# Graph attention and a routed FFN on one core: five conversions and tiny operations of a block's preparation taken off VectorE

## The chip, the cores and the metric

The kernel runs on one core of a Trainium2 chip. The metric is the device time in microseconds of one execution, as a median over runs. PE is TensorE, DVE is VectorE, ACT is ScalarE, POOL is GpSimd, SP is SyncE. A core's engines run their own instruction queues in order and wait for one another by semaphores.

## The reference

Two layers with residuals are computed over 6250 nodes of 256 features and 100000 edges.

```python
x = x + gat(layernorm(x), [src, dst], W_w, W_b, a)       # 2 heads of 128
x = x + ffn(layernorm(x)[None], W1, b1, Wg, bg, Wd, bd)[0]

# gat: Wh = x @ W_w + W_b; s = Wh.a_src, t = Wh.a_dst
#   e = leaky_relu(s[src] + t[dst]); alpha = softmax of e over the edges of one src
#   h'[n] = sum over edges with src == n of alpha * Wh[dst]   (Wh[n] where there is none)
# ffn: H = gelu(x @ W1 + b1); probs = softmax(H @ Wg + bg) over 8 experts
#   out = probs[e] * (H @ Wd[e] + bd[e]) for the expert e of highest probability
```

## The kernel before

**Sorting and projection.** Ahead of the block loop the edges are packed into 31-bit keys (block of 128 sources, destination, source within the block), sorted along each of 128 partitions, and written to memory (`keys`). The nodes are normalised and projected meanwhile and stored in `table`.

**The block loop.** There are 49 blocks of 128 source nodes. For a block, each partition reads a window of its sorted keys (`window`, an indirect DMA on POOL at column `first[:, b]`). `measure` counts on DVE how many keys of the window belong to the block (`c1`), where the next window begins, how many keys are beyond the twelve that a partition handles itself (`over`, in bfloat16), and the destinations of these twelve (`dsti`). `prefix` sums `over` across partitions with three small matmuls on PE, `prefix_out` copies the sums on ACT into `late` and into the last column of `rest`. `split` puts the surplus keys as exact floating-point numbers in the other columns of `rest`, forms the choice matrix `pick`, and the positions `loc` of the twelve. `gather_late` multiplies `pick` with `rest` on PE; `choose` picks out of the product the surplus key of each slot, and adds three more columns to `dsti` and to `loc`. `spread` transposes `loc` on PE, and sends it through memory to be broadcast (`lbc`). `compare` turns `lbc` into one-hot rows, `factors` multiplies them with the source terms on PE and `factor_sums` reduces these.

`fetch` gathers the fifteen rows a partition needs from `table` (15 indirect DMAs of POOL, in three groups of five). For each group `compare_back` forms one-hot columns `hot` on DVE, `weigh` forms the weights on DVE and multiplies them into the rows, with a copy of the weights by ACT at its end (L833), and `add_up` multiplies `hot` with the rows on PE. Edges into the first 256 nodes (the hot ones) are not gathered, but counted (`pick_pairs`, `count_pairs`), weighed (`scale_terms` on ACT, `weigh_pairs` on DVE) and added (`add_pairs` on PE). `finish` divides and adds the residual on DVE.

**The FFN.** Every four finished blocks make a group: `g_norm` on DVE, `g_xn` on ACT, `g_turn` and `g_hidden` on PE with Gelu on ACT, logits, choice of the expert on DVE, and rows sent to their expert's place in memory (`g_rows`, `g_send`). Full tiles of 128 rows of one expert are then loaded (`w_load`), transposed (`w_turn`, with two copies `half` by ACT), multiplied with that expert's weights (`w_expert`: L1150 for the bias and 16 matmuls of L1152 with addresses from registers), and stored.

**The order.** Every step has a slot and a place within it, written by hand, and all instructions are issued in the order of these two numbers. Block b has base `u = 3 * b`; a slot works on several blocks at once.

```python
            at(u - 6, 46, window, b)
            at(u - 4, 24, measure, b)
            at(u - 4, 43, prefix, b)
            at(u - 3, 5, prefix_out, b)
            at(u - 3, 12, split, b)
            at(u - 3, 33.7, gather_late, b)
            at(u - 2, 16, choose, b)
            at(u - 2, 33.5, spread, b)
            at(u, 33, factors, b)
```

`weigh_pairs` of an older block stands at place 13, right behind `split`; `pick_pairs` at 17, right behind `choose`; `w_turn` at 21 and `g_hidden` at 20; `add_up` at 32, before `factors` and `gather_late`; `compare_back` and `weigh` at 48 and 50.

Of the kernel before, what the change touches and what calls it, by code (L numbers as in the profile page):

```python
# [10 lines left out]
F32 = mybir.dt.float32  # L11
BF16 = mybir.dt.bfloat16
I32 = mybir.dt.int32
U16 = mybir.dt.uint16
AF = mybir.ActivationFunctionType
ALU = mybir.AluOpType
# [7 lines left out]
P = 128  # L24


def of_bits(bits):

    return struct.unpack("<f", struct.pack("<I", bits))[0]
# [7 lines left out]
def common_path(  # L37
# [22 lines left out]
    nc = tc.nc  # L60
# [13 lines left out]
    NB = -(-N // P)  # L74
# [5 lines left out]
    HB, HK = 2, 4  # L80
    HOT = HB * P
    ND, NC, WIN = 12, 3, HK + 40
    NR = WIN - HK - ND
    KS = ES + WIN
# [25 lines left out]
    const = ctx.enter_context(tc.tile_pool(name="const", bufs=1))  # L110
# [37 lines left out]
    bd3 = const.tile([3, NX * C], BF16, name="bd3")  # L148


    first_f = const.tile([P, NB + 1], F32, name="first_f")
    nc.gpsimd.iota(first_f[:, 0:1], pattern=[[0, 1]], base=0, channel_multiplier=KS,
                   allow_small_or_imprecise_dtypes=True)
    first = const.tile([P, NB + 1], I32, name="first")
    iota_bf = const.tile([P, HOT], BF16, name="iota_bf")
    nc.vector.tensor_copy(iota_bf, iota_s[:, :HOT])

# [8 lines left out]
    bias = const.tile([P, C], F32, name="bias")  # L166
# [20 lines left out]
    with ExitStack() as edges:  # L187
# [6 lines left out]
        kp = edges.enter_context(tc.tile_pool(name="keyp", bufs=2))  # L194
# [133 lines left out]
        def first_window():  # L328
            few = sp.tile([P, HK], F32, name="few")
            n = sp.tile([P, 1], F32, name="few_n")  # L330
            nc.vector.tensor_scalar(few, bufs[-1][:, :HK], of_bits(0x40000000 + (HOT << 8)), None,
                                    op0=ALU.is_lt, op1=ALU.add, accum_out=n)
            nc.vector.tensor_add(first_f[:, 0:1], first_f[:, 0:1], n)
            nc.vector.tensor_copy(first[:, 0:1], first_f[:, 0:1])

# [176 lines left out]
        for i, (d, flip) in enumerate(steps):  # L514
# [4 lines left out]
            else:  # L519
                early(t, exchange, bufs[i], bufs[i + 1], d, flip)  # L520
        early(t + 1.02, keep_keys)
        early(t + 1.03, first_window)
        for h in range(2):
            early(60 + h, lambda h=h: nc.sync.dma_start(out=empty[:, h * RD // 2:(h + 1) * RD // 2], in_=blank))
# [91 lines left out]
        win, kept, rows, own, sums, res = {}, {}, {}, {}, {}, {}  # L616
# [11 lines left out]
        def measure(b):  # L628


            w = win[b].bitcast(F32)
            mine = kp.tile([P, WIN - HK], F32, name="mine")
            mark = 0x40000000 + ((b + 1) << 21)
            c1 = cnt[:, b:b + 1]
            c2 = kp.tile([P, 1], F32, name="c2")
            nc.vector.tensor_scalar(mine, w[:, HK:], of_bits(mark), None, op0=ALU.is_lt, op1=ALU.add, accum_out=c1)
            nc.vector.tensor_scalar(mine, w[:, HK:], of_bits(mark + (HOT << 8)), None,
                                    op0=ALU.is_lt, op1=ALU.add, accum_out=c2)
            nc.vector.tensor_scalar(c2, c2, c1, float(HK), op0=ALU.subtract, op1=ALU.min)
            nc.vector.scalar_tensor_tensor(first_f[:, b + 1:b + 2], c1, first_f[:, b:b + 1], c2,  # L640
                                           op0=ALU.add, op1=ALU.add)
            nc.vector.tensor_copy(first[:, b + 1:b + 2], first_f[:, b + 1:b + 2])
            over = kp.tile([P, 1], BF16, name="over")
            nc.vector.tensor_scalar(over, c1, float(-ND), 0.0, op0=ALU.add, op1=ALU.max)
            dsti = kp.tile([P, T], I32, name="dsti", bufs=5)
            nc.vector.tensor_scalar(dsti[:, :ND], win[b][:, HK:HK + ND], 8, 0x1FFF,
                                    op0=ALU.logical_shift_right, op1=ALU.bitwise_and)
            kept[b] = {"over": over, "dsti": dsti}
# [11 lines left out]

        def split(b):
            w = win.pop(b)
            rest_i = kp.tile([P, NR], I32, name="rest_i")
            nc.vector.tensor_single_scalar(rest_i, w[:, HK + ND:], 0x1FFFFF, op=ALU.bitwise_and)
            nc.vector.tensor_scalar(kept[b]["rest"][:, :NR], rest_i, float(1 << 21), None, op0=ALU.add)
            pick = kp.tile([P, NS], F32, name="pick", bufs=1)
            nc.vector.tensor_scalar(pick, iota_s, late[:, b, 0:1], None, op0=ALU.is_ge)
            nc.vector.scalar_tensor_tensor(pick, iota_s, late[:, b, 2:3], pick, op0=ALU.is_lt, op1=ALU.mult)

            place_i = kp.tile([P, HK + ND], I32, name="place_i")  # L670
            nc.vector.tensor_single_scalar(place_i, w[:, :HK + ND], 255, op=ALU.bitwise_and)
            loc = kp.tile([P, T], F32, name="loc", bufs=5)
            nc.vector.scalar_tensor_tensor(loc[:, :ND], iota_r[:, :ND], cnt[:, b:b + 1], place_i[:, HK:],
                                           op0=ALU.is_lt, op1=ALU.mult)

            hot_i = kp.tile([P, HK], I32, name="hot_i")
            nc.vector.tensor_single_scalar(hot_i, w[:, :HK], 8, op=ALU.logical_shift_right)
            pair = kp.tile([P, HK], F32, name="pair")
            nc.vector.tensor_scalar(pair, hot_i, float(0x400000 + (b << 13)), None, op0=ALU.subtract)
            kept[b].update(loc=loc, pick=pick, pair=pair, place=place_i)  # L680
# [67 lines left out]
        def choose(b):  # L748
            k = kept[b]
            loc, dsti = k["loc"], k["dsti"]  # L750
            pk = k["pm"][:, :NC * (NR + 1)].rearrange("p (c r) -> p c r", c=NC)
            col = kp.tile([P, NC], F32, name="col")
            nc.vector.tensor_sub(col, slot_of, pk[:, :, NR])
            hit = kp.tile([P, NC, NR], F32, name="hit")
            nc.vector.tensor_tensor(hit, iota_s[:, :NR].unsqueeze(1).to_broadcast([P, NC, NR]),
                                    col.unsqueeze(2).to_broadcast([P, NC, NR]), op=ALU.is_equal)
            nc.vector.tensor_mul(hit, hit, pk[:, :, :NR])
            got = kp.tile([P, NC], F32, name="got")
            nc.vector.tensor_reduce(got, hit, AX.X, ALU.add)
            got_i = kp.tile([P, NC], I32, name="got_i")  # L760
            nc.vector.tensor_copy(got_i, got)
            nc.vector.tensor_scalar(dsti[:, ND:], got_i, 8, 0x1FFF, op0=ALU.logical_shift_right, op1=ALU.bitwise_and)
            nc.vector.tensor_single_scalar(got_i, got_i, 255, op=ALU.bitwise_and)
            nc.vector.tensor_copy(loc[:, ND:], got_i)

        def spread(b):
            k = kept[b]
# [116 lines left out]
        over = fc.tile([1, 1], F32, name="over")  # L884
# [342 lines left out]
        for k in range(NPH):  # L1227
# [26 lines left out]
            n = (TILES if last else max(0, (rows_in - LAG) // P)) - worked  # L1254
# [25 lines left out]
@with_exitstack  # L1280
def gat_then_ffn_kernel(
    ctx: ExitStack,
    tc: tile.TileContext,
    x: bass.AP,
    src: bass.AP,
    dst: bass.AP,
    W: bass.AP,
    Wb: bass.AP,
    a: bass.AP,
    W1: bass.AP,  # L1290
    b1: bass.AP,
    Wg: bass.AP,
    bg: bass.AP,
    Wd: bass.AP,
    bd: bass.AP,
    out: bass.AP,
):
    keep = ctx.enter_context(tc.tile_pool(name="keep", bufs=1))
    odd = keep.tile([1, 1], I32, name="odd")
    common_path(tc, x, src, dst, W, Wb, a, W1, b1, Wg, bg, Wd, bd, out, odd)  # L1300
    flag = tc.nc.values_load(odd[0:1, 0:1], min_val=0, max_val=1,
                             skip_runtime_bounds_check_because="a flag, 0 or 1")
    with tc.If(flag > 0):
        general_path(tc, x, src, dst, W, Wb, a, W1, b1, Wg, bg, Wd, bd, out)
# [506 lines left out]
```

## Time and profile before

| | |
|---|---|
| median of 3 runs | 1692.44 us (1686.08 to 1697.46) |
| the profiled execution | 1684.62 us, of which the span from first to last instruction is 1682.3 us |
| busy | PE 76%, PE's weight load 57%, DVE 65%, ACT 30%, POOL 52% |
| granted TensorE clock, mean | 0.834 |
| DMA | 264.23 MB, mean 157 GB/s |

The busy shares are means over the whole span. In the timeline a line gives start, duration, engine, line and operation; in square brackets stands how long the engine was idle before it, and what ended that. "issue" there is idle time for which the profile shows no wait.

### The profile page before, as it was taken

Reading aid. Unit: us, or ns where it says so; the run is one execution under the profiler, and the core shown is the slowest. Engines: PE = TensorE matmul, PEld = TensorE weight load, DVE = VectorE, ACT = ScalarE, POOL = GpSimd, SP = SyncE. Lnnn points to the kernel's source line nnn. Section 1 sums busy time; section 2 is a strip of 40 time slices with the busy share of each in tenths; the row PEclk is TensorE's granted clock in tenths of the full one; section 3 lists DMA queues with packets and bytes.
Section 4 is the critical chain, followed back from the end, with each engine's and each line's share of the span. In section 5 each row is a group of like instructions: output and inputs, shape, how many; then the busy total and the mean of one; then the engine's idle time right before and its main releaser. Section 6 shows DMA issues by size and latency. Waiting matters only on the chain. (4 is left out here: it accounts for less than half of the span.)

```text
span 1682.3 us, 22169 instructions
## 1 busy us (share of the span) xinstructions
PE 1271.4 (76%) x6405; PEld 958.1 (57%) x6405; DVE 1090.2 (65%) x3765; ACT 511.2 (30%) x1424; POOL 876.6 (52%) x989
## 2 busy tenths in 40 slices
PE   4764765766857878879778778788798787788687
PEld 3543644444545665655656656656556566566576
DVE  7875766476777676776766866766767676654211
ACT  4850211213223223233232232232332332425221
POOL 0026555465656555645656565556466455554343
PEclk9886767877978888979888888789788797889889
DMA  5656545354545455545545554555455444454473
GB/s 167 187 165 168 164 141 161 109 166 139 148 137 160 139 172 158 175 140 159 148 153 163 158 160 134 176 160 166 138 153 168 141 153 140 154 174 159 167 257 105
DMA packets 119213, 264.23 MB, mean 157 GB/s; under 512 B 24988, under 2 KB 65076, under 8 KB 118940
## 3 DMA queue, kind: packets, MB, share of 16 engines
q0 software_dynamic: 47264, 137.46, 27.6%
q1 hardware_dynamic: 64544, 118.23, 21.9%
q10 hardware_dynamic: 7276, 7.03, 1.3%
q8 instruction: 55, 0.90, 0.2%
q14 instruction: 74, 0.61, 0.1%
HBM read 211.45 MB, written 57.90 MB: 160 GB/s over the span
## 5 line engine op out<-in xcount | busy, mean ns | idle before, releaser
L800 POOL DMA_INDIRECT wg<-table,dsti x735 | 715.8, 974 | 416.8 <-issue 266.8
L840 PE MATMUL p_a<-wg,hot 128*128 128x258 f32 x1470 | 391.4, 416 | 76.2 <-ACT wg L833 42.2
L840 PEld LDWEIGHTS p_a<-wg,hot 128*128 128x128 f32 x1470 | 298.7, 209 | 143.4 <-issue 50.0
L923 PE MATMUL pf<-xT,w_sb 128*128 128x512 f32 (+1 forms) x416 | 213.5, 665 | 32.7 <-ACT xT L915 28.9
L832 DVE TENSOR_TENSOR wg<-wg,fix 128x1280 f32<-128x1280 f32 x147 | 218.9, 1489 | 14.0 <-DVE fix L831 8.0
L1152 PE MATMUL pf<-wd_sb,half 128*128 x880 | 221.7, 408 | 0.9 <-issue 0.9
L1152 PEld LDWEIGHTS pf<-wd_sb,half 128*128 128x128 f32 x880 | 174.4, 203 | 43.0 <-issue 13.7
L923 PEld LDWEIGHTS pf<-xT,w_sb 128*128 128x128 f32 x416 | 87.6, 227 | 127.8 <-issue 93.3
L1066 POOL DMA_INDIRECT by_expert<-row,place_i x47 | 46.9, 997 | 186.3 <-ACT row L1060 74.1
L817 DVE TENSOR_TENSOR hot<-fix,loc 128x640 f32<-128x640 f32 x147 | 120.0, 816 | 32.0 <-ACT wg L833 31.7
L1045 ACT COPY row<-pf 128x512 f32<-128x512 f32 x94 | 53.3, 587 | 255.9 <-PE pf L1044 170.3
L746 PE MATMUL pm<-rest,pick 128*128 128x29 f32 x294 | 56.3, 326 | 93.3 <-DVE wt L718 47.2
L710 ACT ACTIVATE wt<-tm,hot_e 128x128 f32<-128x128 f32 x392 | 125.0, 393 | 0.0
L925 ACT ACTIVATE hT<-pf,b_sb 128x512 f32<-128x512 f32 (+1 forms) x104 | 68.1, 662 | 179.0 <-PE pf L923 102.4
L746 PEld LDWEIGHTS pm<-rest,pick 128*128 128x128 f32 x294 | 52.2, 255 | 97.7 <-issue 95.8
L1044 PE MATMUL pf<-ident,hT 128*128 128x128 f32 x392 | 81.8, 355 | 31.9 <-ACT row L1045 19.5
L833 ACT COPY wg<-fix 128x10 f32<-128x10 f32 x147 | 25.2, 172 | 258.1 <-DVE wg L832 138.0
L1045 ACT COPY half<-pf 128x512 f32<-128x512 f32 x110 | 62.3, 585 | 99.8 <-PE pf L1044 48.3
L1044 PEld LDWEIGHTS pf<-ident,hT 128*128 128x128 f32 x392 | 61.3, 185 | 44.2 <-ACT row L1045 25.7
L771 ACT CAST lT<-pm 15x128 bf16<-15x128 f32 x49 | 12.5, 255 | 234.9 <-PE pm L769 174.0
L858 DVE TENSOR_SCALAR den_all<-p_a 128x2 f32<-128x2 f32 (+1 forms) x49 | 7.7, 157 | 114.9 <-PE p_a L840 108.4
L450 PE MATMUL pf<-w_sb,xT 128*128 128x260 f32 x196 | 60.3, 436 | 20.4 <-ACT xT L444 20.3
(274 smaller groups left out, 1875.1 us busy)
## 6 DMA issues: line engine op xcount, KB each, us to landing
row<-by_expert SPq DMA_DIRECT2D x39, 641.0 KB
lbc<-lrow SPq DMA_DIRECT2D x49, 480.0 KB
tm<-terms SPq DMA_DIRECT2D x49, 256.0 KB
wg<-table,dsti POOLq DMA_INDIRECT x735
wg<-by_expert SPq DMA_DIRECT2D x16, 641.0 KB
wd_sb<-in_L_ffn_Wd_dram SPq DMA_DIRECT2D x8, 1024.0 KB
table<-tb ACTq DMA_DIRECT2D x12, 520.0 KB
xs<-in_x_dram SPq DMA_DIRECT2D x12, 512.0 KB
```

The lines of the kernel that those rows point to most:

```text
L450: nc.tensor.matmul(pW[:, :TW], xT[:, k * P:(k + 1) * P], w_sb[:, k, :], start=(k == 0), stop=(k == KC - 1))
L710: nc.scalar.activation(kept[b]["wt"][:, i, g, h, :], tm[:, i, h, :], AF.Identity, scale=hot_e[:, g, i, h:h + 1])
L746: nc.tensor.matmul(pk[:, c, :], k["pick"][:, c * P:(c + 1) * P], k["rest"], start=True, stop=True)
L800: nc.gpsimd.indirect_dma_start(out=wg[:, t - QS[q], :], out_offset=None, in_=table[:, :], in_offset=bass.IndirectOffsetOnAxis(ap=kept[b][" ...
L817: nc.vector.tensor_tensor(hot[:, :n], iota_ps.unsqueeze(1).to_broadcast([P, n, P]), kept[b]["loc"][:, QS[q]:QS[q + 1]].unsqueeze(2).to_bro ...
L832: nc.vector.tensor_mul(wgv[:, :, :, :D], wgv[:, :, :, :D], p_w.unsqueeze(3).to_broadcast([P, n, H, D]))
L840: nc.tensor.matmul(sums[b], hot[:, t - QS[q], :], wg[:, t - QS[q], :SE], start=(t == 0), stop=(t == T - 1))
L923: nc.tensor.matmul(ph[:, :w], wt["w1"][:, k, j * P:(j + 1) * P], xT[:, k, :w], start=(k == 0), stop=(k == KC - 1))
L925: nc.scalar.activation(hT[:, j, :w], ph[:, :w], AF.Gelu, bias=wt["b1"][:, j:j + 1])
L1044: nc.tensor.transpose(pT[:, j * P:(j + 1) * P], rows(4 * h + j), ident)
L1045: nc.scalar.copy(o, pT)
L1152: nc.tensor.matmul(py[:, :C], res[k]["half", i, j // 4][:, j % 4, :], wt["wd"][:, ds(wo[0] + j * C, C)], start=False, stop=(j == KH - 1))
```

## The change

Three functions of a block's preparation change, and the one that finds the first window.

- `first`, the integer column of the next window, is written directly by the operation that computes it. The floating-point copy `first_f` and the conversion after it go, in `measure` and in `first_window`.
- `over` is computed by ACT as Relu(c1 - 12) with a bias tile `minus_nd`, where DVE computed max(c1 - 12, 0).
- In `split` the surplus keys become floating-point numbers by setting the exponent bits (0x4B000000, the value is then 2^23 plus the 21-bit key), in the same operation that masks them, where a second one had added 2^21 and converted.
- In `choose` the bits of the chosen number are used as they are, with no conversion to an integer. The position is masked into a tile of its own, `late_i`, and ACT copies it as a floating-point number into `loc`, where DVE did.

The order of the steps, slots and places stays as it is.

```diff
-    first_f = const.tile([P, NB + 1], F32, name="first_f")
-    nc.gpsimd.iota(first_f[:, 0:1], pattern=[[0, 1]], base=0, channel_multiplier=KS,
+    row_at = const.tile([P, 1], F32, name="row_at")
+    nc.gpsimd.iota(row_at, pattern=[[0, 1]], base=0, channel_multiplier=KS,
                    allow_small_or_imprecise_dtypes=True)
     first = const.tile([P, NB + 1], I32, name="first")
+    minus_nd = const.tile([P, 1], F32, name="minus_nd")
+    nc.gpsimd.memset(minus_nd, float(-ND))
...
-            nc.vector.tensor_add(first_f[:, 0:1], first_f[:, 0:1], n)
-            nc.vector.tensor_copy(first[:, 0:1], first_f[:, 0:1])
+            nc.vector.tensor_add(first[:, 0:1], row_at, n)
...
-            nc.vector.scalar_tensor_tensor(first_f[:, b + 1:b + 2], c1, first_f[:, b:b + 1], c2,
+            nc.vector.scalar_tensor_tensor(first[:, b + 1:b + 2], c1, c2, first[:, b:b + 1],
                                            op0=ALU.add, op1=ALU.add)
-            nc.vector.tensor_copy(first[:, b + 1:b + 2], first_f[:, b + 1:b + 2])
             over = kp.tile([P, 1], BF16, name="over")
-            nc.vector.tensor_scalar(over, c1, float(-ND), 0.0, op0=ALU.add, op1=ALU.max)
+            nc.scalar.activation(over, c1, AF.Relu, bias=minus_nd)
...
-            rest_i = kp.tile([P, NR], I32, name="rest_i")
-            nc.vector.tensor_single_scalar(rest_i, w[:, HK + ND:], 0x1FFFFF, op=ALU.bitwise_and)
-            nc.vector.tensor_scalar(kept[b]["rest"][:, :NR], rest_i, float(1 << 21), None, op0=ALU.add)
+            nc.vector.tensor_scalar(kept[b]["rest"].bitcast(I32)[:, :NR], w[:, HK + ND:], 0x1FFFFF, 0x4B000000,
+                                    op0=ALU.bitwise_and, op1=ALU.bitwise_or)
...
-            got_i = kp.tile([P, NC], I32, name="got_i")
-            nc.vector.tensor_copy(got_i, got)
+            got_i = got.bitcast(I32)
             nc.vector.tensor_scalar(dsti[:, ND:], got_i, 8, 0x1FFF, op0=ALU.logical_shift_right, op1=ALU.bitwise_and)
-            nc.vector.tensor_single_scalar(got_i, got_i, 255, op=ALU.bitwise_and)
-            nc.vector.tensor_copy(loc[:, ND:], got_i)
+            late_i = kp.tile([P, NC], I32, name="late_i")
+            nc.vector.tensor_single_scalar(late_i, got_i, 255, op=ALU.bitwise_and)
+            nc.scalar.copy(loc[:, ND:], late_i)
```

## The prediction

> **What bounds the kernel now.** I read the page's busy shares first, then busy time by stretch, then the groups of the lines that change, then the instructions in order of time over one period of the block loop.
>
> ```profile
> PE 1271.4 (76%) x6405; PEld 958.1 (57%) x6405; DVE 1090.2 (65%) x3765; ACT 511.2 (30%) x1424; POOL 876.6 (52%) x989
> ...
> 900.00:1100.00 200.00, 161.41 (x862) 124.96 (x860) 141.46 (x488) 58.96 (x162) 115.09 (x121) 0.83 0.50 153
> ...
> 926.00:947.00 21.00, 14.76 (x88) 11.95 (x86) 17.87 (x64) 5.65 (x17) 13.44 (x14) 0.97 0.63 197
> 947.00:959.00 12.00, 9.58 (x43) 8.07 (x44) 10.05 (x35) 2.72 (x6) 4.82 (x5) 0.50 0.24 66
> ```
>
> Columns of the stretches: length, then PE, PEld, DVE, ACT, POOL busy with counts, clock, DMA share, GB/s. No engine is full. Over 200 us of the loop PE has 161 and DVE 141, so the bound changes hands along in-order queues. Two stretches of one period show it: from 926 to 947 DVE is busy 17.9 of 21 us and PE only 14.8; right after, PE works at clock 0.50.
>
> The loop repeats every four blocks: `choose` starts its first removed conversion at 811.77 and again at 927.92, 116.15 us later. Between the first `choose` (about 119 us) and the last (1480 us) the pattern settled after about 165 us, so (1480-165)/116.15 = 11.3 periods count.
>
> What the change touches, in the groups by line (name of the operation, then busy us and mean ns):
>
> ```profile
> L761 DVE CAST got_i<-got 128x3 int32<-128x3 f32 x49 | 11.2, 228 | 1.7
> L665 DVE TENSOR_SCALAR rest<-rest_i 128x28 f32<-128x28 int32 x49 | 8.9, 181 | 5.1 <-DVE rest_i L664 3.5
> L764 DVE CAST loc<-got_i 128x3 f32<-128x3 int32 x49 | 8.8, 180 | 1.7
> L642 DVE CAST first<-first_f 128x1 int32<-128x1 f32 x49 | 7.5, 154 | 2.1 <-DVE first_f L640 0.5
> L644 DVE TENSOR_SCALAR over<-cnt 128x1 bf16<-128x1 f32 x49 | 7.2, 146 | 0.0
> ...
> L659 ACT COPY rest<-late 128x1 f32<-128x1 f32 x49 | 9.4, 192 | 1.5
> ...
> L462 ACT ACTIVATE tb<-tb,low 128x8 f32<-128x8 f32 (+1 forms) x13 | 3.9, 302 | 0.4
> ```
>
> And how they stand in time (start, duration, engine, line), in the timeline:
>
> ```profile
> 927.64 0.24 DVE L759 TENSOR_REDUCE got<-hit 128x3 f32<-128x84 f32 x1
> 927.92 0.23 DVE L761 CAST got_i<-got 128x3 int32<-128x3 f32 x1
> 928.18 0.17 DVE L762 TENSOR_SCALAR dsti<-got_i 128x3 int32<-128x3 int32 x1
> 928.38 0.17 DVE L763 TENSOR_SCALAR got_i<-got_i 128x3 int32<-128x3 int32 x1
> 928.59 0.17 DVE L764 CAST loc<-got_i 128x3 f32<-128x3 int32 x1
> 928.66 0.87 DVE L686 TENSOR_SCALAR dests<-iota_bf,pair 128x256 bf16<-128x256 bf16 x4
> ...
> 935.76 1.05 ACT L1045 COPY half<-pf 128x512 f32<-128x512 f32 x2
> ...
> 936.13 0.15 DVE L644 TENSOR_SCALAR over<-cnt 128x1 bf16<-128x1 f32 x1
> ...
> 936.38 0.16 PE L654 MATMUL pf<-over,before_bf 128*128 128x1 bf16 x1 [0.74 <-ACT lg L991]
> ...
> 937.28 0.26 PE L1150 MATMUL pf<-bd,ones_bf 3*128 x1 [0.69 <-issue]
> ...
> 859.50 1.45 PE L746 MATMUL pm<-rest,pick 128*128 128x29 f32 x6 [4.08 <-DVE wt L718]
> ```
>
> See two things. Dependent DVE operations start 0.20 to 0.28 us apart, an independent one 0.07 to 0.09 us after the one before (L764 to L686). And PE waits 4.08 us before `gather_late` (L746) until DVE is through with `split` and `weigh_pairs`.
>
> **What the Trainium skill says.** "VectorE: DVE Perf Modes", § Rules for kernel authors: for chained small operations, lower their count, fusing for its own sake does not help. The trace agrees in part: a dependent operation is worth 0.2 to 0.28 us whatever its three columns hold, an independent one less than half of that. "ScalarE: Activation LUTs", § Table sets: relu and copy lie in every table set, so `Relu` between `Gelu` and `Exp` should load nothing. For Copy and Identity the trace agrees (13 table loads for Gelu, 13 for Exp, none between for hundreds of copies); no Relu runs in it. "TensorE: Matmul & The Clock Gate", Part 1: PE falls to half clock after an idle window of about 3.4 us and comes back after a busy one. The trace agrees on the two levels (0.50 and 0.97 to 1.00 in the stretches).
>
> **The change part by part.**
>
> *measure.* L642 goes (L640 writes the integer itself), L644 goes to ACT. In the timeline L640 starts at 935.80, L642 at 936.05, L644 at 936.13, L646 (dsti) at 936.19 to 936.22. Now L646 follows L640 as an independent operation, 0.15 us later as after other operations of 0.23 us (L673 at 943.31, L677 at 943.46): 935.95, so about 0.25 us less on DVE.
>
> *split.* L664 and L665 become one operation. They start at 941.75 and 941.96, L667 at 942.05; now L667 starts about 0.09 after the one: 0.21 us less. I price the fused two-step integer operation like L646, also two bit operations (190 ns mean).
>
> *choose.* The conversion L761 goes: 0.26 us. L763 no longer overwrites what L762 reads, so it may start 0.08 instead of 0.20 after it: 0.12. L764 leaves: 0.20. Together 0.58 us between L759 and L686.
>
> Sum on DVE: 1.04 us a block, x49 = 51 us of its queue (43.6 by the busy times above). That is the ceiling.
>
> *On ACT.* `over` as Relu with a bias operand: nearest row L462, 302 ns; `loc` as a copy: L659, 192 ns. 0.49 x 49 = 24 us more, on an engine at 30%: hidden unless its place in the queue hurts. `loc` stands behind the weight copy L833 of the third group, before the next block work; PE's reader, the transpose L769 in `spread`, comes after ten matmuls of `add_up` that need that same copy, so 0.2 us more disappear there. What now queues behind `loc`'s wait for DVE are Gelu and `half` copies; followed through the timeline, from the fifth period on the next ACT instruction began 1.2 to 8.8 us after the old L764 had ended, so the wait holds up nothing (three earlier blocks by 1.7 us at most). `over` has a worse place in one block of four: ACT is in the two `half` copies until 936.81, so `over` would end at about 937.1 against 936.28 today, 0.85 us later. PE reads it at the head of its queue (L654, which waits already), with the expert's L1150 and L1152 and the next `add_up` behind it. The L1152 matmuls need those `half` copies anyway, but L1150's 0.69 us of issue time would then start later. Bounds: 0 to 0.85 us a period on PE; I take 0, because PE then still waits 1.9 us in the factor products and 1.3 us for DVE at L746 before the block is over. Elsewhere PE comes to L654 at least 1 us after `over` would end.
>
> *Prologue.* One conversion fewer before the first window, one memset more on POOL: 0.2 us, nothing.
>
> *What lies on the path.* Walking the waits back through 834 to 950 us: `measure` lies on it in three of the four blocks (before the norm of a group at 847, at 881 and at 936), `split` in two (888, 942), `choose` in one (928). Elsewhere PE or ACT carries it. 3 x 0.25 + 2 x 0.21 + 0.58 = 1.75 us a period, x11.3 = 20 us at most. Part goes to what is late next. Block at 847: 0.25 in full, PE idles 4.08 us there. Block at 881 to 892: 0.46 saved, but PE had only 1.06 us of idle time, and between 893 and 896 PE, DVE, POOL and SyncE all have issue gaps (PE 0.55 and 1.82 us) that I expect to stay: I take 0.2. Stretch 926 to 947: 1.04 saved; issue gaps again at the end, I take 0.8. Together 1.25 x 11.3 = 14 us.
>
> Against the profiled execution, 1684.6 us (span 1682.3): 1670.5. That execution lay 7.8 us under the median of the runs, 1692.44; carried over to the median, 1678.
>
> **The rivals.**
>
> *PE takes over.* At 80% busy, half of it after clock drops, PE could absorb all but the block with the 4.08 us gap and a little more: 0.4 x 11.3 = 4.5 us, 1688. For it: the whole-engine issue gaps and the 4.5 us of DVE waiting for PE before 926.8 us. Against: DVE at 85% in the stretch after.
>
> *The clock pays twice.* The stretch at clock 0.50 after 947 follows PE's idle time before L746. If that idle time, shortened by about 1 us, no longer costs one window of 3.4 us at half clock, PE gains 1.7 us more a period: (1.25 + 1.7) x 11.3 = 33 us, 1659. For it: PE is on the path right there. Against: the gap before L746 stays over 2 us with the factor products' own wait.
>
> *Slower: PE stands behind `over`.* In the block with the `half` copies PE's wait at L654 grows from 0.74 to about 1.6 us; 0.85 x 11.3 = 9.6 us if PE carries the path from there, and if that idle time costs a half-clock window, another 1.7 x 11.3 = 19. Of 29, 14 are paid by the gains: +15, 1707. It decides once PE's slack of about 2 to 3 us before L746 is used up, which a faster DVE shortens. Against: that slack.
>
> *Relu does load a table.* Then it doesn't do what it says: at 1283 ns a load (row of L925's loads) and two for each block, 98 x 1.28 = 126 us on ACT, perhaps a third on the path: +42 less 14, 1720. The table-set section speaks against it.
>
> **How the numbers follow.** Forecast as summed 0.46; PE takes over 0.24; clock pays twice 0.18; behind `over` 0.08; table loads 0.04. One per cent is 17 us, about what a measurement of this kernel can tell from no change. Faster by over 1% means under 1675.5: the clock case and 0.4 of the forecast's, 0.37. Slower by over 1% (over 1709): the table case and part of `over`, 0.08. The rest 0.55. Range: from 1656 (clock case, nearly whole) to 1697 (PE takes over with the runs' spread of 6 us, and a little of `over`).
>
> **What would show it.** Right: DVE busy down by 40 to 45 us with 246 instructions fewer (five a block and one ahead); L646 0.15 us after L640; `choose` 0.6 us shorter; ACT up by 22 to 26 us and 98 instructions; still 28 table loads or fewer; the period near 114.9 us; PE's idle time before L746 down. Wrong: the period unchanged with PE's idle time moved to L654 or to L1044; the granted clock under 0.82; waits of Gelu or `half` on the two new ACT lines.

## The result and the profile after

| | before | after |
|---|---|---|
| median of the compared runs | 1689.64 us (6 runs, 1680.82 to 1697.46) | 1671.2 us (6 runs, 1656.3 to 1677.36) |
| profiled execution, span | 1684.62 us, 1682.3 us | 1677.36 us, 1675.6 us |
| mean granted clock | 0.834 | 0.830 |

The ratio is 0.9888, 95% interval [0.9844, 0.9932]: 18.5 us less, where 14 were forecast. The same change measured twice more, beside other kernels, gave 0.9894 and 0.9917. The ratios here and below leave out runs more than 1.5% above the fastest of the same kernel; the medians keep them, so the two can differ by a thousandth.

The busy line of the page of the kernel after, then its busy time by stretch (the columns are those of the same view of before: length, PE, PEld, DVE, ACT, POOL with counts, clock, DMA share, GB/s):

```profile
PE 1269.7 (76%) x6405; PEld 952.3 (57%) x6405; DVE 1048.9 (63%) x3519; ACT 529.2 (32%) x1522; POOL 881.1 (53%) x990
```

```profile
926.00:947.00 21.00, 14.70 (x74) 11.26 (x73) 17.35 (x61) 6.03 (x19) 13.22 (x14) 0.92 0.67 196
947.00:959.00 12.00, 9.29 (x46) 8.02 (x47) 9.13 (x30) 2.81 (x7) 5.10 (x5) 0.57 0.23 66
900.00:1100.00 200.00, 159.91 (x867) 123.22 (x865) 136.54 (x456) 61.50 (x175) 116.61 (x122) 0.86 0.51 155
```

VectorE has 41.3 us and 246 instructions less, ScalarE 98 more. PE's work is what it was. The pattern of the stretches stays too: the stretch after 947 still runs at little more than half clock.

The rows that took the place of the removed ones, in the groups by line of the kernel after (busy us, mean ns, then idle time just before and what ended it), with two of the table loads. The numbers of most lines in the block loop are one less than before:

```profile
L924 ACT ACT_TABLE_LOAD x13 | 16.7, 1283 | 1.3 <-PE pf L922 1.0
L990 ACT ACT_TABLE_LOAD x13 | 16.7, 1283 | 0.2
...
L644 ACT ACTIVATE over<-cnt,minus_nd 128x1 bf16<-128x1 f32 x49 | 14.4, 295 | 5.7 <-DVE mine L637 3.5 <-DVE st L864 0.7 <-issue 0.4
...
L641 DVE SCALAR_TENSOR_TENSOR first<-cnt,c,first 128x1 int32<-128x1 f32 x49 | 10.8, 220 | 1.7
...
L763 ACT CAST loc<-late_i 128x3 f32<-128x3 int32 x49 | 9.9, 202 | 130.4 <-DVE late_i L762 62.9 <-DVE got L758 33.8 <-DVE hit L756 25.3
...
L663 DVE TENSOR_SCALAR rest<-win 128x28 int32<-128x28 int32 x49 | 8.8, 179 | 0.0
```

Each of the two operations that write their final type directly (L641 at 220 ns, L663 at 179 ns) costs what one of its two predecessors cost. The new ScalarE rows are at 295 and 202 ns. The 130 us of idle time ahead of L763 are no loss by themselves: ScalarE is busy a third of the time and would have stood somewhere.

The same period as before the change in the timeline of the kernel after (start, duration, engine, line; idle time before it in brackets):

```profile
927.34 0.24 DVE L758 TENSOR_REDUCE got<-hit 128x3 f32<-128x84 f32 x1
927.61 0.23 DVE L760 TENSOR_SCALAR dsti<-got 128x3 int32<-128x3 int32 x1
927.69 0.16 DVE L762 TENSOR_SCALAR late_i<-got 128x3 int32<-128x3 int32 x1
927.76 0.87 DVE L685 TENSOR_SCALAR dests<-iota_bf,pair 128x256 bf16<-128x256 bf16 x4
927.88 0.19 ACT L763 CAST loc<-late_i 128x3 f32<-128x3 int32 x1 [5.67 <-issue]
...
934.86 1.05 ACT L1044 COPY half<-pf 128x512 f32<-128x512 f32 x2
934.89 0.22 DVE L641 SCALAR_TENSOR_TENSOR first<-cnt,c,first 128x1 int32<-128x1 f32 x1
935.03 0.30 DVE L646 TENSOR_SCALAR dsti<-win 128x12 int32<-128x12 int32 x1
...
935.80 0.31 ACT L644 ACTIVATE over<-cnt,minus_nd 128x1 bf16<-128x1 f32 x1
936.16 0.16 PE L654 MATMUL pf<-over,before_bf 128*128 128x1 bf16 x1 [0.49 <-ACT over L644]
...
937.27 0.26 PE L1149 MATMUL pf<-bd,ones_bf 3*128 x1 [0.90 <-issue]
...
943.09 0.69 DVE L717 TENSOR_TENSOR wt<-wt,pm 128x512 f32<-128x512 f32 x1
943.19 0.47 PE L786 MATMUL pm<-src_term,lbc 128*128 128x12 bf16 x13
...
946.28 0.17 PE L786 MATMUL pm<-src_term,lbc 128*128 128x12 bf16 x1 [2.62 <-remote]
946.30 0.18 DVE L830 TENSOR_TENSOR fix<-fe 128x10 f32<-128x10 f32 x1 [1.70 <-remote]
...
947.68 0.17 PE L786 MATMUL pm<-src_term,lbc 128*128 128x12 bf16 x1 [1.23 <-issue]
...
947.71 1.35 PE L745 MATMUL pm<-rest,pick 128*128 128x29 f32 x6
```

From `got` to the first `dests` are 0.42 us, before they were 1.02. In this one period the end of `weigh_pairs` (L717) came 16.4 us after `got`, before 18.7: VectorE was 2.3 us earlier. And yet PE reached `gather_late` (L745) 20.4 us after `got`, before 19.5: it spent the time inside the factor products (L786), in idle time that ends with no wait that the profile can name, while VectorE stood still as well at 946. So one period taken alone can hide the gain or show the opposite. I therefore took all periods: the start of PE's `gather_late` with its idle time before it, mean of blocks 8 to 46 by the block's number modulo 4, from two traces of before and three of after:

| PE idle before `gather_late`, us | blocks 0 mod 4 | 1 | 2 | 3 | sum |
|---|---|---|---|---|---|
| before (two traces) | 0.75, 0.60 | 0.25, 0.30 | 1.76, 1.71 | 4.06, 4.02 | 6.8, 6.6 |
| after (three traces) | 0.12, 0.18, 0.05 | 0.59, 0.45, 0.67 | 1.14, 1.26, 1.20 | 3.94, 3.93, 3.94 | 5.8, 5.8, 5.9 |

That is 0.9 us a period less on PE at this place, the same in all three traces. It is not the only place that changed. Take as the loop the eleven periods from the `choose` of block 3 to that of block 47. Over it PE's idle time was 293 and 290 us before, and 286, 278 and 271 after. Ahead of `gather_late` it fell by 11 us on the mean, ahead of `add_up` by 13 us (58 and 49 to 40 or 41), and ahead of the matmuls of `count_pairs` it rose by 9 us (17 and 20 to 27 to 29).

What VectorE no longer had to do turned mostly into waiting. These are waits of VectorE, before and after (us in total, times, longest):

```profile
DVE den_all L858 <- PE p_a L840: 108.4, 30, 5.5
...
DVE hot L817 <- ACT wg L833: 31.7, 15, 3.5
```

```profile
DVE den_all L857 <- PE p_a L839: 116.9, 32, 6.4
...
DVE hot L816 <- ACT wg L832: 43.2, 15, 4.6
```

The other traces agree: 111 and 35 us before, 119 to 121 and 45 to 46 after. Over the loop VectorE's idle time rose from 389.5 and 380.8 us in two traces of before to 416.4, 414.8 and 413.3 in three of after. Its work there fell by 38 us (875 to 837): 30 of them came back as waiting, 8 as time.

The loop took 1264.3 and 1255.8 us before, 1253.2, 1252.7 and 1250.0 after: 8 us less on the mean, with 8 us between the two traces of before. The stretch behind the last `choose` is unchanged (203 and 206 us before, 201 to 203 after). The profiled executions thus show less than half of the difference of the medians. They are single executions: both profiles of before fell below the medians of before beside them, and two of the three of after above theirs. So the size of the gain is read from the compared runs, and the traces show which waits changed.

### The profile page after: what moved, and what is told of

Same layout as the page of the kernel before. It is cut to its first block, busy times and chain, and to the rows that moved or that the text cites. A ratio compares the mean times of both kernels' runs of the same rounds, so it can differ in the third digit from the quotient of the medians.

```text
span 1675.6 us, 22023 instructions
## 1 busy us (share of the span) xinstructions
PE 1269.7 (76%) x6405; PEld 952.3 (57%) x6405; DVE 1048.9 (63%) x3519; ACT 529.2 (32%) x1522; POOL 881.1 (53%) x990
## 5 line engine op out<-in xcount | busy, mean ns | idle before, releaser
L922 PE MATMUL pf<-xT,w_sb 128*128 128x512 f32 (+1 forms) x416 | 217.8, 675 | 35.4 <-ACT xT L914 33.4
L1151 PE MATMUL pf<-wd_sb,half 128*128 x880 | 217.3, 403 | 0.1
L745 PE MATMUL pm<-rest,pick 128*128 128x29 f32 x294 | 52.2, 314 | 80.2 <-DVE wt L717 41.9
L745 PEld LDWEIGHTS pm<-rest,pick 128*128 128x128 f32 x294 | 48.3, 240 | 85.2 <-issue 83.5
L1043 PE MATMUL pf<-ident,row 128*128 128x128 f32 x312 | 57.4, 325 | 29.3 <-issue 9.2
L623 POOL DMA_INDIRECT win<-keys,first x49 | 53.8, 1098 | 39.8 <-DMA keys<-keyb 14.2
```

The costliest lines, as they stand in the source:

```text
L623: nc.gpsimd.indirect_dma_start(out=win[b], out_offset=None, in_=keys[:, :], in_offset=bass.IndirectOffsetOnAxis(ap=first[:, b:b + 1], axis=1))
L745: nc.tensor.matmul(pk[:, c, :], k["pick"][:, c * P:(c + 1) * P], k["rest"], start=True, stop=True)
L922: nc.tensor.matmul(ph[:, :w], wt["w1"][:, k, j * P:(j + 1) * P], xT[:, k, :w], start=(k == 0), stop=(k == KC - 1))
L1043: nc.tensor.transpose(pT[:, j * P:(j + 1) * P], rows(4 * h + j), ident)
L1151: nc.tensor.matmul(py[:, :C], res[k]["half", i, j // 4][:, j % 4, :], wt["wd"][:, ds(wo[0] + j * C, C)], start=False, stop=(j == KH - 1))
```

## The experiments

Two theories stood against each other. The path theory, that of the prediction: VectorE's queue decides in some stretches of a period, and a microsecond taken from it there is a microsecond gained. Its rivals: PE or the idle time without a wait decides, and VectorE's savings vanish; or the two moves to ScalarE cost PE something at `over`, and the three conversions carry the gain alone.

The first four ran together on one chip on which the kernel before takes 1433.39 us, not 1690. The ratios below are all to the kernel before on the same chip.

**The three conversions alone.** The change with `over` and the last step of `loc` back on VectorE:

```
-            nc.scalar.activation(over, c1, AF.Relu, bias=minus_nd)
+            nc.vector.tensor_scalar(over, c1, float(-ND), 0.0, op0=ALU.add, op1=ALU.max)
...
-            nc.scalar.copy(loc[:, ND:], late_i)
+            nc.vector.tensor_copy(loc[:, ND:], late_i)
```

> The changed kernel with over and the last step of loc back on VectorE: only the three conversions that vanish altogether are gone. It saves about 0.77 of the 1.05 us a block of VectorE's queue. Path theory (VectorE time in measure, split and choose lies on the path, and counts wherever it is taken off): three quarters of the change's gain, ratio to before about 0.992. Rival, the moves to ScalarE cost (PE stands behind over): as fast as the whole change or faster, 0.989 or less.

Measured: 1414.57 us, 0.9864 [0.9835, 0.9894], 19.5 us less. The conversions take some 0.8 us a block from VectorE's queue, 39 us in 49 blocks; half of it arrived in the time. That is more than the path theory gave them, and the value that the rival had named (0.989 or less). Taken alone it would speak for the rival; the next experiment decides. The three conversions were not taken away one by one, so how much each brings is not shown.

**The two moves alone.** The kernel before, with only these two operations on ScalarE:

```
-            nc.vector.tensor_scalar(over, c1, float(-ND), 0.0, op0=ALU.add, op1=ALU.max)
+            nc.scalar.activation(over, c1, AF.Relu, bias=minus_nd)
...
-            nc.vector.tensor_copy(loc[:, ND:], got_i)
+            nc.scalar.copy(loc[:, ND:], got_i)
```

> The kernel before with the two moves to ScalarE alone (over as Relu, loc's last copy). Path theory: 0.28 of 1.05 us a block, some 5 us, ratio 0.997. Rival, the moves cost: 1.000 to 1.006, with PE's wait before the prefix matmuls over 10 us longer in sum.

Measured: 1428.08 us, 0.996 [0.9942, 0.9979]. The moves help a little, and the rival's 1.000 to 1.006 lies outside the interval. That PE has to stand behind `over` is true, as a wait: in this kernel PE's waits have the line

```profile
PE pf L656 <- ACT over L646: 19.2, 14, 5.0
```

while with `over` on VectorE (the kernel of the experiment before) it read

```profile
PE pf L654 <- DVE over L644: 9.8, 7, 5.4
```

That is about 9 us more of waiting for `over`. Some of it took the place of other idle time: all of PE's idle time ahead of these three matmuls is 14.9 us in the kernel with `over` on VectorE and 19.2 us in this one. The whole is still faster, so this wait doesn't reach the end of the kernel in full. The slower rival fell here, on this chip; on the other kind the two moves were not run alone.

**A pad ahead of the division, in every block.** The change with five dependent additions of one column (0.9 us in the trace) in `finish`, ahead of `den_all`, where VectorE waits for PE longest:

```
+            for _ in range(5):
+                nc.vector.tensor_scalar(pad, pad, 0.0, None, op0=ALU.add)
             nc.vector.tensor_scalar(den_all[:r, b, :], p_a[:r, D:D2], TINY, None, op0=ALU.max)
```

> The changed kernel with five dependent one-column additions on VectorE at the start of finish's division, about 1 us a block, where VectorE waits for PE's sums (117 us in 32 of the 49 blocks). Path theory: hidden in most blocks, within 5 us of the changed kernel, ratio to before 0.988 to 0.993. Rival, VectorE's load as such sets the time: the gain is gone, 0.998 to 1.002.

Measured: 1428.94 us, 0.997 [0.9953, 0.9987]. That lies above what I expected, and the interval reaches the rival's 0.998. Against the kernel of the next experiment (0.985), which has no pad, it is 0.012 or 17 us. My error was to take the wait as evenly spread. The waits at `den_all`, first in the kernel of the next experiment, then with the pad:

```profile
DVE den_all L857 <- PE p_a L839: 74.9, 29, 5.8
```

```profile
DVE den_all L859 <- PE p_a L839: 55.4, 18, 6.0
```

The pads take 44 us in 49 blocks, and the wait became only 19.5 us shorter. Without the pad, once the loop has settled, the blocks of number 1 mod 4 wait 3.8 us and more there, those of 2 mod 4 about 1 us, every second one of 0 mod 4 about 1.4 us, and those of 3 mod 4 next to nothing. So in roughly half of the blocks no wait was there to take the pad up. That led to the pair of pads below.

**The fill of `by_expert` a slot later.** To see whether the transfers that begin with it cause the idle time without a wait:

```
-                at(26 + 12 * (NX - e), 80, lambda e=e:
+                at(27 + 12 * (NX - e), 80, lambda e=e:
```

> The changed kernel with the nine fills of an expert's first rows (by_expert<-empty, 656 KB each) issued one slot later on SyncE. In the stretch where VectorE gained most, all engines then stood still for some 4 us while the DMA engines were full with such a fill and the loads of own and tm. Theory, this traffic makes the stall and swallows the gain: 9 x 1.5 to 2 us less, ratio to before 0.978 to 0.981. Rival, the stall belongs to the instructions there and not to the fill: as the changed kernel, 0.987 to 0.991, and the stall stays in the trace.

Measured: 1413.19 us, 0.985 [0.9819, 0.9882]. The interval leaves out the theory's 0.978 to 0.981 and reaches into the rival's range. The change alone was not run on this chip; the two halves above multiply to 0.9864 x 0.996 = 0.9825. So nothing speaks for the later fill here, and it was tried again on the other kind of chip (below). This chip turned out to be no place for the question: over the loop PE stands idle without a wait for 0 to 4 us, where the traces from the slower chips have 108 to 140.

The next four ran together on a chip on which the kernel before takes 1684.71 us.

**The change itself.**

> The changed kernel as it is, so that the other runs have it beside them on their chip. Path theory: with VectorE at three quarters of the span here, the gain is between the sum of the two parts (0.9864 and 0.996 give 0.9825) and the size found first (0.9888); 0.985 expected. If the fill a slot later was worth anything, this is slower than its 0.985 by 0.01.

Measured: 1666.08 us, 0.9894 [0.9854, 0.9933]. That is above the 0.985 I expected, and near the 0.9888 found first.

**The same pad where VectorE waits, and where it doesn't.** Twelve of the small additions, planned as 2.4 us and 2.2 us in the traces, in every fourth block: 12 blocks, 26.6 us of VectorE's queue in both kernels, in the first in the blocks that wait at `den_all`, in the second in those that don't:

```
+            for _ in range(12 if b % 4 == 1 else 0):      # second kernel: b % 4 == 3
+                nc.vector.tensor_scalar(pad, pad, 0.0, None, op0=ALU.add)
```

> The changed kernel with twelve dependent one-column additions on VectorE ahead of finish's division, some 2.4 us, in the blocks whose number leaves 1 by four. There VectorE waits 3.8 to 5.8 us for PE's sums at that place. Path theory: hidden, as the changed kernel, within 0.003. Rival, VectorE's load as such: 12 x 2.4 = 29 us of load, at the 0.35 us of time for each us of load of the earlier pad 10 us, so slower than the changed kernel by 0.007.

> The same twelve additions, in as many blocks, of those whose number leaves 3 by four: there VectorE does not wait before the division (0 to 0.1 us). Path theory: 12 x 2 to 2.4 us = 24 to 29 us slower than the changed kernel, or 0.017 to 0.020. Rival, load as such: the same as with the pad in the waiting blocks, 0.007.

Measured: 1678.3 us, 0.9958 [0.9932, 0.9984] in the waiting blocks, 1696.49 us, 1.0074 [1.0043, 1.0106] in the others. Against the change beside them the first is slower by 0.006, 11 us, with intervals that just touch, and the second by 0.018, 30 us: all of the pad. The 0.006 is more than the path theory allowed (0.003) and near the 0.007 that the load as such should have cost; but then the second kernel should have cost the same 0.007. The intervals of the two kernels lie apart, so the place counts. The waits at `den_all` show why: without a pad, with it in the waiting blocks, and with it in the others:

```profile
DVE den_all L857 <- PE p_a L839: 121.1, 32, 6.3
```

```profile
DVE den_all L859 <- PE p_a L839: 93.0, 30, 4.7
```

```profile
DVE den_all L859 <- PE p_a L839: 125.2, 32, 6.7
```

In the second line the wait is 28 us shorter than in the first (24 and 26 us against the two other traces of the change), so the pad went into it; in the third it is no shorter. The same load on the same engine costs all of itself or, by the ratios, about 40%, by its place alone. With the intervals the cheaper place could cost anything from 3 to 19 us, and why it costs anything stays open.

**The norm behind the prefix.** To give PE's 4 us ahead of `gather_late` in the blocks 3 mod 4 back, the norm's step `g_xn`, which stands ahead of `prefix_out` in ScalarE's queue, was moved behind `prefix_out`, except in the last group:

```
-                at(v + 0.5 * i, 52, g_xn, k, i)
+                at(*((v + 0.5 * i, 52) if last else (v + 1, 6 + 0.1 * i)), g_xn, k, i)
```

> The changed kernel with the four activations of g_xn placed behind prefix_out on ScalarE (slot v + 1, place 6), for all groups but the last. Today late waits behind them once in four blocks, and PE idles about 4 us before gather_late in those. Theory, that wait is what is left of the path there: late comes 1 to 1.3 us earlier, 11 to 14 us less in 11 to 12 groups, ratio to the changed kernel 0.990 to 0.992. Rival, something else (split and weigh_pairs, the broadcast lbc) ends last there: within 0.002 of the changed kernel.

Measured: 1672.77 us, 0.9921 [0.9897, 0.9944]: not better than the change. PE's idle time in those blocks did shrink, from 3.86 to 2.57 us at the median, here and in the trace of both orders below. PE's whole idle time in the loop did not: 295 and 282 us in these two traces, 271 to 286 in those of the change. The idle time was visible and moved, and gave nothing.

The last four ran on a chip of this kind again, the kernel before at 1689.79 us.

**The change once more, the later fill, both orders, and the kernel before under the profile.** The edits are those shown; "both orders" is the later fill and the norm behind the prefix together.

> The changed kernel as it is, once more beside the others. On a chip where the kernel before takes near 1690 us: 0.987 to 0.991 again. On one where it takes near 1430 us (no idle time there that belongs to no wait): 0.982 to 0.986, the sum of the two parts measured there.

> The changed kernel with the nine fills by_expert<-empty a slot later, beside the changed kernel on the same chip. Theory, the fills' traffic makes the engines stand still where VectorE had gained most: on a chip with such stalls 9 x 1.5 to 2 us, or 0.008 to 0.011 under the changed kernel; on one without them, within 0.003. Rival, the stalls are not the fills': within 0.003 on either, and the idle time without a wait stays in the trace.

> The changed kernel with the fills a slot later and g_xn behind prefix_out. If what ended the gain of the shorter wait before gather_late was PE's own work, within 0.003 of the kernel with the fills moved alone; if it was the stall, 0.005 or more under it.

> The kernel before as it is, for its trace on this chip. With stalls (near 1690 us): 70 us and more of VectorE's idle time in the loop belongs to no wait; without (near 1430 us): next to none, with the same instructions and durations of VectorE.

Measured: the change 1673.69 us, 0.9917 [0.9883, 0.9951], at the edge of what was expected; with the later fill 1676.77 us, 0.9925 [0.9899, 0.9951]; with both orders 1672.66 us, 0.9899 [0.9854, 0.9943]; the kernel before, one execution, 1681.57 us. The fill theory fell: with the fill a slot later PE still stands 127 us of the loop idle without a wait. Neither of the two variants is told apart from the change. In the trace of before, 82 us of VectorE's idle time in the loop end with no wait (10 us) or with one that the profile can't name ("remote", 72 us). The 70 us and more that were expected are there only if both are counted. That trace also gave the second value of before in the numbers above, and a caution: PE's idle time without a wait was 119.7 us in one trace of before and 124.2 in the other, 107.8, 126.7 and 112.7 in three of the change. It differs between two executions of one kernel by as much as between the kernels, so no part of the gain is read from it.

## Why the prediction was right, and where a step was off

The forecast (1678, within 1656 to 1697) was met by 1671.2 us, and by its own mechanism: part of VectorE's shorter queue lies on the path. The conversions alone, which in the loop change only VectorE's work, gained on the faster chip, and on a slower one a pad on VectorE in blocks without a wait cost all of itself. The forecast gain of 14 us lies inside the interval of the measured one, 11.5 to 26.4 us. The measured 1.1% is a little more than the 1% from which the prediction counted a gain as clear; it had given that a chance of 0.37.

*VectorE's steps: right.* Read as medians over the blocks: `measure` L640 to `dsti` 386 to 136 ns, `split` 286 to 82, `got` to `dests` 1021 to 423: 0.25 + 0.20 + 0.60 = 1.05 us a block, worked out as 1.04. L646 follows L641 by 0.14 us, as an independent operation. What the Trainium skill says in "VectorE: DVE Perf Modes", § Rules for kernel authors, to lower the count of operations, held here with this addition: half of the 0.60 us in `choose` came from breaking a dependence and shifting a step to another engine, not from dropping the conversion.

*ScalarE: the price was right, the sign in the page off.* 295 and 202 ns were priced at 302 and 192, 0.49 us together. The sum of durations rose by 23.9 us, as worked out; the busy time by 18.0 only, outside the 22 to 26 I named. Busy time counts overlapping instructions once: the Trainium skill, "ScalarE: Activation LUTs", § What ACT_TABLE_LOAD costs, gives an overlap of some 93 ns between ACTIVATEs back to back. The trace shows about 0.11 us: `over` at 935.80 starts before the second `half` copy ends at 935.91. In the trace after, 58 of the 98 new instructions overlap a neighbour, by 6.5 us in sum, which is about the missing 5.9 us. The same section's price for an ACTIVATE with a bias tile, 280 ns and 0.833 ns a column, stands at 295 here.

*Table loads: right.* 28 before and after; the rival that Relu loads a table is out.

*`over` behind the `half` copies: the order was as foreseen, the delay was not.* I put `over` behind both copies, 0.85 us late. It does run right behind them, at 935.80, but after `got` both copies come 0.60 us earlier than before (7.52 us instead of 8.12), as much as `choose` became shorter. PE starts the prefix 8.82 us after `got`, before 8.74: 0.1 us late. The 0.90 us of issue time of L1149 then came anyway, so PE was at 937.27 as before at 937.28. Over the run PE's wait for `over` grew from 8.0 and 8.4 us to 11.8, 13.7 and 14.0, but all of PE's idle time ahead of these matmuls did not: 16.8 and 16.0 us before, 14.5, 16.1 and 14.5 after. In these traces the wait took the place of others, so taking nothing for it, with 9.6 as the bound, held.

*What lies on the path: the sum was near, its terms were not.* By PE's idle time before `gather_late` (the table above):

- the block with the 4 us gap: 0.25 us taken in full, 0.1 found on the mean;
- the block at 881 to 892 (0 mod 4): 0.2 taken, 0.56 found. PE now hardly waits here, so I would expect little from another microsecond on VectorE in it (not run);
- the stretch 926 to 947 (2 mod 4): 0.8 taken, 0.53 found, and in the one profiled period the opposite;
- the blocks 1 mod 4: nothing taken, 0.3 us more idle time found.

0.1 + 0.56 + 0.53 - 0.3 = 0.9 us a period, against 1.25. It is the same in three traces, but idle time of PE at one place is no measure of the path: with the norm behind the prefix it fell by another 1.6 us a period, and nothing was gained. So it isn't shown in which blocks the gain lies, and that the sum of terms came near is in part luck. The period fell by 0.7 us in the traces (8 of 1260 us over 11 periods), 1.2 were named; the compared runs put it higher, 18.5 / 11.3 = 1.6 us, if all of it lies in the loop. The sign "period near 114.9 us" could not have told: the 116.15 us it started from are one period, and the mean of before was already 1264.3 / 11 = 114.9 us in the same trace, against 113.6 to 113.9 after.

*"PE takes over": true in part.* In the blocks 0 and 1 mod 4 PE idles before `gather_late` 0.1 to 0.7 us. The end of the path's gain on VectorE may be near there; no run tested it. Elsewhere VectorE is still on the path: the pads in `finish` of the blocks 3 mod 4, 26.6 us, cost 30.

*"The clock pays twice": not seen.* The time at half clock in the loop was 445.1 and 429.7 us before, 444.2, 450.6 and 454.7 after, and the mean clock of the three traces after was 0.827 to 0.830. The loop is shorter at a clock no better. The idle time before L745 in the blocks 3 mod 4 stayed at 3.9 us.

Still open are the share of each conversion and of each block in the gain, the cause of the idle time without a wait on the chips of the slower kind, and the ratio of the whole change on the faster one.

## What to carry to other kernels

Chained tiny operations are priced by their start-to-start distance, which the timeline shows, and by whether each depends on the one before; their durations say less. Then ask of each block of a repeating pattern, one at a time, whether the engine waits anywhere behind the saving before the next hand-over: the same 26.6 us cost 30 us or about 11 by that alone. And when single periods scatter by more than the change can bring (109 to 119 us in the trace of before), take the size of the gain from compared runs, and look for its place in means over all periods of several traces: as a hint only, which an edit at that place has to confirm.

## What the runs showed of the hardware

The same kernel took 1433 us on one chip and 1685 to 1690 us on the chips of the other runs. The waits of PE in the kernel with the two moves, on the first, have this as the largest line that ends in "issue" (idle time for which the profile shows no wait):

```profile
PE pf L1152 <- issue: 3.7, 5, 0.8
```

and the kernel before on a chip of the other kind has

```profile
PE p_a L840 <- issue: 33.5, 27, 7.2
...
PE pm L746 <- issue: 33.0, 22, 4.1
```

On the slower kind PE and VectorE stop at once, as at 946 us above: of VectorE's idle time in the loop, 73 to 118 us end with no wait or with one that the profile can't name, and none in the four traces from the faster chip. PE's mean granted clock was 0.83 there and 0.90 on the faster one. PE's busy time, 1160.7 us for the kernel with the three conversions on the faster chip against 1270 us and more for the change, makes up 110 us of the difference, and the rest lies in idle time. The change gained 18.5, 17.9 and 14.0 us in three measurements on the slower kind; on the faster its two parts gained 19.5 and 5.7 us, and the whole was not run there.
